# Last batch of a gated WKV and binary FFN: two groups' partial sums leave PSUM early, alpha within PSUM, biases regrouped

## The chip, the cores and the metric

The kernel runs on one core of one Trainium2 chip. The core has TensorE (matmuls, into PSUM), VectorE, ScalarE and GpSimd (elementwise work), and SyncE, which here only issues DMAs. GpSimd issues DMAs too; those that add into their destination go through it. Sixteen DMA engines serve all of them. The metric is the device time of one execution in microseconds (us); less is better. Times are medians of several runs. A profile is one further execution, recorded by the hardware profiler.

## The reference

Cut to what matters:

```python
# x, kv: (4, 1024, 1024); cond: (4, 256); w, u, bias: (1024,); weight: (1024, 1024); r = x, k = v = kv
tf    = sigmoid(sum(cond, -1))[:, None, None]
decay = exp(-exp(w)) * (0.5 + 0.5 * tf)
ek, ekv = exp(min(k, 30)), exp(min(k, 30)) * v
nf, df  = forward scans  a = a * decay + ekv,  b = b * decay + ek     # along the 1024 rows
nb, db  = the same backward
euk   = exp(min(u + k, 30))
base  = sigmoid(r) * (nf + nb - ekv + euk * v) / max(df + db - ek + euk, 1e-8)
gated = base * (0.8 + 0.2 * tf)
bw    = where(weight >= 0, 1, -1) * alpha       # alpha: mean |weight| of each output row
out   = x + gated @ bw.T + bias
```

## The kernel before

A step `g` is one batch and one block of 128 channels: 4 batches times 8 blocks are 32 steps (`steps`, 0 to 31). TensorE transposes the block so that channels lie on partitions; VectorE scans it forward and backward (L366, L379); ScalarE does exponentials and reciprocals; GpSimd and VectorE the products. The finished block is split into a rounded high part (`act_hi`, L433, ScalarE) and the remainder (`lo_part`, L438, GpSimd), and both are multiplied by the signs of the weights, `wT`. So every product counts two matmuls for each of the 8 blocks.

The order of every engine's work is written out by hand (`manual_schedule`): instructions stand on each engine's queue as they stand in the code, and an engine waits at the first whose inputs or buffers aren't ready. DMAs of SyncE and of GpSimd stand in those queues too.

The first three batches are multiplied channel block by channel block, turned back, put into `staged` tiles and stored. Their x is added afterwards by DMAs from GpSimd that accumulate from x in DRAM into the output in DRAM (`add_x`, L137 to L142, 1 MB each). Four of these twelve are left for the end (`adds[steps]`).

The last batch is multiplied the other way round: rows on partitions. It has 8 groups `n` of 128 rows, each with two halves (`part`) of 512 columns; one half takes 16 matmuls of 512 columns. Each group's x rows are loaded by `load_x_rows` (L477). Since a product over all 8 blocks needs the last step, most of it is left to the end, but the blocks that exist are multiplied as soon as PSUM has a bank for them: `pe_wide_product(n, part, blocks)` (L525). The banks come from `ps_o` (three of 512 columns), `ps_k`, `ps_g` (two each) and `bank`; groups 0 and 5 take both halves of the `ps_k` tile, group 3 of the `ps_g` tile, which also holds the transposed gate `sgT` of the step (L272). In step 30 two halves of group 1 get five blocks, in step 31 further groups get six.

After the last step's elementwise work (L801 to L818) the remaining two blocks follow for groups 0 to 3 (`waiting`, L822), and then groups 4 to 7 from the beginning. A finished half leaves PSUM by `leave_columns` (L536): VectorE multiplies it with `alpha_rows` into an SBUF tile `z` (L539) and adds this to the x rows (L541); then `dve_add_bias` (L530) adds `bias_rows` to a whole group, and SyncE stores it (`finish_wide`, L550). The last group goes in pieces of 512, 256 and 256 columns. `alpha_rows` and `bias_rows` are rows spread over all partitions by a DMA (`load_along_rows`, L494).

Buffers matter for the order of the loads: the gate pool has four tiles, which the x rows of some groups take over once TensorE has transposed their gate; the `eu` pool has three, which are free once the products of their step are done (the last with `num_product`, L419, of the last step's second half); `resid` has two (`staged` tiles). SyncE's queue at the end holds: bias_rows, x rows of groups 4, 5, 6, 7, then the stores. GpSimd's holds the two DMAs that add `euk` to `num` (L384), the product L419 of step 30, and the four `add_x`.

Of the kernel before, what the change touches and what calls it, by code (L numbers as in the profile page):

```python
# [9 lines left out]
F32 = mybir.dt.float32  # L10
# [11 lines left out]
def kernel(  # L22
# [27 lines left out]
    nc = tc.nc  # L50
    P = 128
    B, T, C = x.shape
    TD = time_emb.shape[1]
    NT = T // P
    NC = C // P
    H = 512
# [5 lines left out]
    rows = ctx.enter_context(tc.tile_pool(name="rows", bufs=2))  # L62
    gate_rows = ctx.enter_context(tc.tile_pool(name="gate_rows", bufs=4))
# [13 lines left out]
    sg_rows = {}  # L77
# [59 lines left out]
    def add_x(b, n):  # L137

        rows = slice(2 * n * P, 2 * (n + 1) * P)
        nc.gpsimd.dma_start(  # L140
            out=out[b, rows, :], in_=x[b, rows, :], accum_op=ALU.add, max_dma_last_dim=8192
        )  # L142
# [265 lines left out]
    def act_reciprocal(g, ts=slice(0, T)):  # L408
        b, cc = divmod(g, NC)
        rec = eus[g][:, ts]  # L410
        nc.scalar.activation(  # L411
            rec, rec, AF.Exp, scale=-1.0, bias=ln_g[:, b, cc : cc + 1]
        )
# [13 lines left out]
    def gated_product(g, ts=slice(0, T), engine=nc.gpsimd):  # L427
        engine.tensor_mul(nums[g][:, ts], dens[g][:, ts], nums[g][:, ts])  # L428
# [48 lines left out]
    def load_x_rows(n, pool, tag):  # L477
        t = pool.tile([P, C], F32, tag=tag, name=f"x_rows_{n}")
        nc.sync.dma_start(out=t, in_=x[last, n * P : (n + 1) * P, :])
        x_rows[n] = t  # L480
# [13 lines left out]
    def load_along_rows(pool, tag, name, values):  # L494
        t = pool.tile([P, C], F32, tag=tag, name=name)
        nc.sync.dma_start(out=t, in_=values.unsqueeze(0).to_broadcast([P, C]))
        return t
# [12 lines left out]
            t = ps_o.tile([P, H], F32, tag="po", name=f"wide_{n}_{part}")  # L510
            wide[n, part] = t

    def pe_wide_columns(t, n, cols, blocks):
        h, s = divmod(n, PER)
        for cc in blocks:
            for i in range(2):
                nc.tensor.matmul(  # L517
                    t,
                    gated[last, cc, h][:, i, s * P : (s + 1) * P],
                    wT[:, cc, cols],  # L520
                    start=(cc == 0 and i == 0),
                    stop=(cc == NC - 1 and i == 1),
                )

    def pe_wide_product(n, part, blocks):  # L525
        if (n, part) not in wide:
            open_wide(n, part)
        pe_wide_columns(wide[n, part], n, columns(part), blocks)

    def dve_add_bias(n):  # L530
        nc.vector.tensor_add(x_rows[n], x_rows[n], bias_rows)

    def columns(part):
        return slice(part * H, (part + 1) * H)

    def leave_columns(ps, n, cols):  # L536
        width = cols.stop - cols.start
        t = work.tile([P, width], F32, tag="z", name=f"wide_{n}_{cols.start}")
        nc.vector.tensor_mul(t, ps, alpha_rows[:, cols])  # L539
        xs = x_rows[n][:, cols]  # L540
        nc.vector.tensor_add(xs, xs, t)  # L541

    def leave_wide(n, part):
        leave_columns(wide[n, part], n, columns(part))

    def store_wide(n, part):
        rows = out[last, n * P : (n + 1) * P, columns(part)]
        nc.sync.dma_start(out=rows, in_=x_rows[n][:, columns(part)])

    def finish_wide(n):  # L550
        dve_add_bias(n)
        nc.sync.dma_start(out=out[last, n * P : (n + 1) * P, :], in_=x_rows[n])

    def act_leave(q):
        if q % 2 == 0:
# [61 lines left out]
    with tc.manual_schedule():  # L617
# [39 lines left out]
        def done():  # L657
            while fresh:
                ready.append(fresh.pop(0))

        def scale():
            while ready:
                scaled.append(ready.pop(0))
                act_scale(scaled[-1])

        def turn():
            if scaled:
                leaving.append(scaled.pop(0))
                pe_turn(leaving[-1])

        def leave():
            if leaving:
                act_leave(leaving.pop(0))

        for g in range(steps):
# [19 lines left out]
            if final:  # L695
                done()
            scale()
            done()
            if g > 1:
                act_hi(g - 2, 0)  # L700
                act_hi(g - 2, 1)
            product(parts[g][0])
            if final:
                pe_wide_product(2, 0, range(NC - 3))
            turn()
            if g > 0:
# [46 lines left out]
            leave()  # L753
            done()
            scale()
            if final:
                pe_wide_product(0, 1, range(NC - 2))
            product(parts[g][2])
            if g == steps - 2:
                pe_wide_product(1, 0, range(NC - 3))  # L760
            if g > 0:
                dve_newton_gate(g - 1)
            if g > 0 and not final:
# [7 lines left out]
                load_gate(g + 4)  # L771
            product(parts[g][3])
            turn()
            if parts[g][4]:
                done()
            product(parts[g][4])
            if g == steps - 2:
                pe_wide_product(1, 1, range(NC - 3))
            if final:
                gate = num_pool.tile([P, T], F32, tag="num", name="gate_of_last")  # L780
                nc.scalar.copy(gate, sg_ps[g])
                sg_ps[g] = gate
            leave()
            backward(g, dens[g], "edge_den")
            if not final:
# [4 lines left out]


        g = steps - 1
        bias_rows = load_along_rows(own, "euk", "bias_rows", bias)
        load_x_rows(4, gate_rows, "sg_rows")
        for i in adds[steps]:
            add_x(*i)

        for i in ((2, 1), (3, 0), (3, 1)):
            pe_wide_product(*i, range(NC - 2))

        for ts in halves:  # L801
            dve_denominator(g, ts)
# [2 lines left out]
            act_log(g, ts)  # L805
        for ts in halves:
            act_reciprocal(g, ts)
        gated_product(g - 1, engine=nc.vector)
        for h in range(NH):
            act_hi(g - 1, h)  # L810
        for h, ts in enumerate(halves):
# [4 lines left out]
            act_hi(g, h)  # L816
            lo_part(g - 1, h, nc.vector)
            lo_part(g, h, nc.vector)  # L818
        for n in range(5, NT):
            load_x_rows(n, eu_pool, "eu")  # L820

        waiting = [(n, part) for n in range(4) for part in range(2)]  # L822
        for i in waiting:
            pe_wide_product(*i, range(NC - 2, NC))
        for i in waiting:
            leave_wide(*i)
        biased = iter((0, 4, 1, 5, 2, 6, 3))
        for n in range(4, NT - 1):
            for part in range(2):
                pe_wide_product(n, part, range(NC))  # L830
                if n != 5:
                    leave_wide(n, part)
                    finish_wide(next(biased))

            for part in range(2 if n == 5 else 0):
                leave_wide(n, part)
                finish_wide(next(biased))
        dve_add_bias(NT - 1)
        finish_wide(next(biased))
        n = NT - 1  # L840
        for cols, pool, tag in (
            (slice(0, H), ps_o, "po"),
            (slice(H, 3 * H // 2), ps_o, "po"),
            (slice(3 * H // 2, C), ps_k, "kT"),
        ):
            bank_of = pool.tile([P, cols.stop - cols.start], F32, tag=tag, name=f"last_{cols.start}")
            pe_wide_columns(bank_of, n, cols, range(NC))
            leave_columns(bank_of, n, cols)
            nc.sync.dma_start(
                out=out[last, n * P : (n + 1) * P, cols], in_=x_rows[n][:, cols]  # L850
            )


# [28 lines left out]
```

## Time and profile before

| what | value |
|---|---|
| time, median of 3 runs | 489.85 us (489.81 to 491.19) |
| time of the profiled execution | 489.83 us |
| its span, first to last instruction | 488.0 us |
| VectorE busy | 474.9 us (97%) |
| GpSimd busy | 402.2 us (82%) |
| TensorE matmuls busy | 363.9 us (75%) |
| ScalarE busy | 335.9 us (69%) |
| DMA, SyncE's queue (q1) | 59.78 MB, 41.0% of 16 engines |
| DMA, GpSimd's queue (q0) | 29.37 MB, 31.6% of 16 engines |
| the 12 accumulating DMAs of 1 MB | 11.8 us from issue to landing (median) |

Shares are of the whole span. The time is 1.83 us more than the span. The page divides the span into stages only by its 40 slices; what happens in the last 60 us is read from the trace with a window: the chain of what ended last there, each engine's timeline, and the DMA queues' share of the 16 engines. An instruction's entry gives its start in us from the span's start, its length, its engine and line, and, in brackets, how long its engine stood idle before it and what ended that.

### The profile page before, as it was taken

What the parts mean: (1) busy time and instruction counts of PE and PEld (TensorE: products, weight loads), DVE (VectorE), ACT (ScalarE), POOL (GpSimd) and SP (SyncE); (2) the same over time, 40 slices, a digit from 0 to 9 for tenths busy, and PEclk for the clock granted to TensorE, in tenths of its full rate; (3) what the DMA queues carried; (4) which work ended last, traced back from release to release, by engine and by line L of the source; (5) the groups of instructions that cost most, each with busy time, mean ns of one, the idle gap of its engine ahead of it and who ended that gap; (6) DMA issues with size and microseconds to landing.
All of it is one profiled execution on the core that took longest, in us unless ns stands there. A gap on an engine that the chain in (4) does not pass through costs nothing.

```text
span 488.0 us, 5214 instructions
## 1 busy us (share of the span) xinstructions
PE 363.9 (75%) x1813; PEld 296.9 (61%) x1813; DVE 474.9 (97%) x331; ACT 335.9 (69%) x466; POOL 402.2 (82%) x276
## 2 busy tenths in 40 slices
PE   3434433344588877778999998965999998989996
PEld 2333332233466666656777777744888777868885
DVE  6999999999999999999999999999999999999976
ACT  4795968869595967769697879697866979724000
POOL 3379999999999999999999999999999999991000
PEclk9975566666699999999999999985999999999999
DMA  8865565555455555559787996889569697899954
GB/s 227 246 173 146 156 174 141 137 141 140 112 147 150 147 141 139 147 139 254 177 208 161 264 235 173 167 213 221 126 108 277 151 271 213 188 229 284 235 198 176
DMA packets 89762, 89.49 MB, mean 183 GB/s; under 512 B 2660, under 2 KB 80776, under 8 KB 88200
## 3 DMA queue, kind: packets, MB, share of 16 engines
q1 hardware_dynamic: 83320, 59.78, 41.0%
q0 software_dynamic: 6400, 29.37, 31.6%
q8 instruction: 14, 0.23, 0.2%
q14 instruction: 12, 0.10, 0.1%
q10 hardware_dynamic: 16, 0.00, 0.0%
HBM read 55.59 MB, written 29.36 MB: 174 GB/s over the span
## 4 chain that ended last, share of the span: by engine, by line
DVE 75%; PE 17%; issue 3%; ACT 2%; POOL 0%; DMA 0%; SPq 0%; DVEq 0%; POOLq 0%; ACTq 0%
DVE num L379 13%; DVE den L379 13%; DVE den L366 13%; DVE num L366 12%; PE wide L517 8%; DVE den L389 7%; DVE num L350 6%; DVE den L423 6%; PE po L449 5%; DVE euk L356 4%; PE last L517 2%; PE bank L517 1%; PE sgT L272 1%; PE turned L469 1%; PE kT L266 1%
## 5 line engine op out<-in xcount | busy, mean ns | idle before, releaser
L449 PE MATMUL po<-gated,wT 128*128 128x512 f32 x768 | 199.7, 408 | 0.3 <-ACT staged L557 0.3
L449 PEld LDWEIGHTS po<-gated,wT 128*128 128x128 f32 x768 | 141.9, 192 | 30.4 <-ACT staged L557 0.8
L266 PE MATMUL kT<-ident,k_rows 128*128 128x128 f32 x248 | 42.1, 325 | 61.6 <-issue 43.0
L272 PE MATMUL sgT<-ident,sg_rows 128*128 128x128 f32 x256 | 43.2, 324 | 46.4 <-DVE den L423 41.2
L438 POOL TENSOR_TENSOR gated<-num,gated 128x512 fp32r<-128x512 f32 x60 | 75.6, 1280 | 2.4
L266 PEld LDWEIGHTS kT<-ident,k_rows 128*128 128x128 f32 x248 | 33.8, 167 | 69.4 <-issue 51.6
L379 DVE TENSOR_TENSOR_SCAN den<-bank,edge_den,den 128x1024 f32<-128x1024 f32 x32 | 74.8, 2339 | 0.4 <-ACT edge_den L372 0.4
L416 POOL TENSOR_TENSOR den<-den,eu 128x1024 f32<-128x1024 f32 x31 | 73.8, 2380 | 1.4 <-ACT eu L411 1.4
L379 DVE TENSOR_TENSOR_SCAN num<-bank,edge_num,num 128x1024 f32<-128x1024 f32 x32 | 74.8, 2337 | 0.0
L419 POOL TENSOR_TENSOR num<-num,eu 128x1024 f32<-128x1024 f32 x31 | 73.7, 2377 | 0.8 <-DMA num<-euk 0.8
L428 POOL TENSOR_TENSOR num<-den,num 128x1024 f32<-128x1024 f32 x30 | 71.8, 2393 | 2.8 <-DVE den L423 0.5
L366 DVE TENSOR_TENSOR_SCAN den<-bank,den 128x1024 f32<-128x1024 f32 x32 | 72.2, 2258 | 0.0
L366 DVE TENSOR_TENSOR_SCAN num<-bank,num 128x1024 f32<-128x1024 f32 x31 | 70.6, 2277 | 0.0
L272 PEld LDWEIGHTS sgT<-ident,sg_rows 128*128 128x128 f32 x256 | 35.1, 167 | 57.1 <-DVE den L423 29.7
L433 ACT CAST gated<-num 128x512 fp32r<-128x512 f32 x64 | 36.5, 618 | 30.2 <-POOL num L428 25.8
L396 POOL TENSOR_SCALAR den<-den,floor 128x1024 f32<-128x1024 f32 x31 | 36.8, 1188 | 20.7 <-DVE den L389 17.5
L404 ACT ACTIVATE eu<-den,gain 128x1024 f32<-128x1024 f32 (+1 forms) x33 | 36.9, 1121 | 20.8 <-POOL den L396 20.4
L517 PE MATMUL wide<-wT,gated 128*128 128x512 f32 x192 | 45.4, 393 | 2.1 <-POOL gated L438 2.1
L557 ACT COPY staged<-turned 128x512 f32<-128x512 f32 x48 | 27.5, 574 | 21.3 <-PE turned L469 21.3
L517 PEld LDWEIGHTS wide<-wT,gated 128*128 128x128 f32 x192 | 35.8, 188 | 10.2 <-POOL gated L438 2.5
L389 DVE SCALAR_TENSOR_TENSOR den<-eu,top,den 128x1024 f32<-128x1024 f32 (+1 forms) x33 | 41.5, 1260 | 0.0
L356 DVE SCALAR_TENSOR_TENSOR euk<-eu,top,kT 128x1024 f32<-128x1024 f32 x31 | 38.7, 1250 | 0.0
(91 smaller groups left out, 578.9 us busy)
## 6 DMA issues: line engine op xcount, KB each, us to landing
sg_rows<-in_x_dram SPq DMA_DIRECT2D x32, 512.0 KB, 5.9
num<-euk POOLq DMA_DIRECT2D x32, 512.0 KB, 5.6
k_rows<-in_fside_BxSxS_dram SPq DMA_DIRECT2D x31, 512.0 KB, 5.2
out_dram<-staged SPq DMA_DIRECT2D x24, 512.0 KB, 5.1
out_dram<-in_x_dram POOLq DMA_DIRECT2D x12, 1024.0 KB, 11.8
w_rows<-in_L_ffn_weight_dram SPq DMA_DIRECT2D x8, 512.0 KB, 5.7
x_rows<-in_x_dram SPq DMA_DIRECT2D x8, 512.0 KB, 11.5
out_dram<-x_rows SPq DMA_DIRECT2D x7, 512.0 KB, 2.6
```

What stands on the lines that cost most here:

```text
L266: nc.tensor.transpose(kT[:, s * P : (s + 1) * P], k_rows[g][:, s, :], ident)
L272: nc.tensor.transpose(t[:, s * P : (s + 1) * P], sg_rows[g][:, s, :], ident)
L356: nc.vector.scalar_tensor_tensor(euk, eus[g], top[:, b, cc : cc + 1], k_ps[g], ALU.min, ALU.mult)
L366: nc.vector.tensor_tensor_scan(t, decay_row(g), t, 0.0, ALU.mult, ALU.add)
L379: nc.vector.tensor_tensor_scan(back, decay_row(g), back, inits[g, which], ALU.mult, ALU.add)
L389: nc.vector.scalar_tensor_tensor(dens[g][:, ts], eus[g][:, ts], top[:, b, cc : cc + 1], dens[g][:, ts], ALU.min, ALU.add,)
L416: engine.tensor_mul(dens[g][:, ts], dens[g][:, ts], eus[g][:, ts])
L419: engine.tensor_mul(nums[g][:, ts], nums[g][:, ts], eus[g][:, ts])
L428: engine.tensor_mul(nums[g][:, ts], dens[g][:, ts], nums[g][:, ts])
L438: engine.tensor_sub(t[:, 1, :], nums[g][:, h * H : (h + 1) * H], t[:, 0, :].bitcast(F32))
L449: nc.tensor.matmul(prods[q], wT[:, cc, oc * P : (oc + 1) * P], gated[b, cc, h][:, i, :], start=(cc == 0 and i == 0), stop=(cc == NC - 1 an ...
L517: nc.tensor.matmul(t, gated[last, cc, h][:, i, s * P : (s + 1) * P], wT[:, cc, cols], start=(cc == 0 and i == 0), stop=(cc == NC - 1 and i ...
```

## The change

Group 6 (`begun`) is multiplied in two parts. Five of its eight blocks (`pe_partial`, both halves) go into step 30; ScalarE copies each half into one SBUF tile `partial`, taken from `resid` (`act_partial`), so that the bank comes free. At the end GpSimd adds the bias to group 6's x rows, multiplies `partial` by alpha and adds it to the x rows; the four `add_x` DMAs stand behind these three in its queue. The other three blocks of group 6 are the last work of TensorE, in pieces of 512, 256 and 256 columns (`rest`). Other products of the early blocks move: (1, 0) within step 30, (1, 1) from step 30 to 31, (0, 1) behind the last gate transpose.

`leave_columns` multiplies by alpha within PSUM and adds from PSUM to the x rows. The other bias additions are put between the groups: 0 and 1 after (4, 0), 4 after (4, 1), 5 and 7 after group 5, 2 and 3 after (7, 0).

The copy of the last step's gate from PSUM (`gate_of_last`) moves behind the reciprocals on ScalarE. On SyncE's queue, group 6's x rows come ahead of group 4's; bias_rows, so far first, comes last, behind the x rows of 5 and 7, in the third `eu` tile, which group 7 had. The stores follow in the order 0, 1, 4, 5, 2, 3, 7, 6.

```diff
-    def pe_wide_columns(t, n, cols, blocks):
+    def pe_wide_columns(t, n, cols, blocks, ends=(0, NC - 1)):
...
-                    start=(cc == 0 and i == 0),
-                    stop=(cc == NC - 1 and i == 1),
+                    start=(cc == ends[0] and i == 0),
+                    stop=(cc == ends[1] and i == 1),
...
     def leave_columns(ps, n, cols):
-        width = cols.stop - cols.start
-        t = work.tile([P, width], F32, tag="z", name=f"wide_{n}_{cols.start}")
-        nc.vector.tensor_mul(t, ps, alpha_rows[:, cols])
+        nc.vector.tensor_mul(ps, ps, alpha_rows[:, cols])
         xs = x_rows[n][:, cols]
-        nc.vector.tensor_add(xs, xs, t)
+        nc.vector.tensor_add(xs, xs, ps)
...
+    begun = NT - 2
+    partial_ps = {}
+    partials = []
+
+    def pe_partial(part):
+        t = ps_o.tile([P, H], F32, tag="po", name=f"partial_{part}")
+        pe_wide_columns(t, begun, columns(part), range(NC - 3), (0, NC - 4))
+        partial_ps[part] = t
+
+    def act_partial(part):
+        if part == 0:
+            partials.append(resid.tile([P, C], F32, tag="x_res", name="partial"))
+        nc.scalar.copy(partials[0][:, columns(part)], partial_ps[part])
...
             scale()
+            if final:
+                act_partial(1)
             done()
...
             product(parts[g][0])
             if final:
+                pe_wide_product(1, 1, range(NC - 3))
                 pe_wide_product(2, 0, range(NC - 3))
...
-            if final:
-                pe_wide_product(0, 1, range(NC - 2))
             product(parts[g][2])
             if g == steps - 2:
-                pe_wide_product(1, 0, range(NC - 3))
+                pe_partial(0)
...
             turn()
+            if g == steps - 2:
+                leave()
+                act_partial(0)
+                pe_partial(1)
...
             if g == steps - 2:
-                pe_wide_product(1, 1, range(NC - 3))
-            if final:
-                gate = num_pool.tile([P, T], F32, tag="num", name="gate_of_last")
-                nc.scalar.copy(gate, sg_ps[g])
-                sg_ps[g] = gate
+                pe_wide_product(1, 0, range(NC - 3))
...
         g = steps - 1
-        bias_rows = load_along_rows(own, "euk", "bias_rows", bias)
-        load_x_rows(4, gate_rows, "sg_rows")
-        for i in adds[steps]:
-            add_x(*i)
-
-        for i in ((2, 1), (3, 0), (3, 1)):
-            pe_wide_product(*i, range(NC - 2))
+        for n in (begun, 4):
+            load_x_rows(n, gate_rows, "sg_rows")
...
             act_reciprocal(g, ts)
+        gate = num_pool.tile([P, T], F32, tag="num", name="gate_of_last")
+        nc.scalar.copy(gate, sg_ps[g])
+        sg_ps[g] = gate
+        for i in ((0, 1), (2, 1), (3, 0), (3, 1)):
+            pe_wide_product(*i, range(NC - 2))
...
-        for n in range(5, NT):
+        for n in (5, 7):
             load_x_rows(n, eu_pool, "eu")
+
+        bias_rows = load_along_rows(eu_pool, "eu", "bias_rows", bias)
+
+        def add_bias(n, engine=nc.vector):
+            engine.tensor_add(x_rows[n], x_rows[n], bias_rows)
...
+        add_bias(begun, nc.gpsimd)
+        nc.gpsimd.tensor_mul(partials[0], partials[0], alpha_rows)
+        nc.gpsimd.tensor_add(x_rows[begun], x_rows[begun], partials[0])
+        for i in adds[steps]:
+            add_x(*i)
...
-        biased = iter((0, 4, 1, 5, 2, 6, 3))
-        for n in range(4, NT - 1):
-            for part in range(2):
-                pe_wide_product(n, part, range(NC))
-                if n != 5:
-                    leave_wide(n, part)
-                    finish_wide(next(biased))
...
+        for n, part, biased in (
+            (4, 0, (0, 1)), (4, 1, (4,)), (5, 0, ()), (5, 1, (5, 7)), (7, 0, (2, 3)), (7, 1, ())
         ):
+            pe_wide_product(n, part, range(NC))
+
+            for i in ((0, 1) if part else ()) if n == 5 else (part,):
+                leave_wide(n, i)
+            for i in biased:
+                add_bias(i)
+                if i != 7:
+                    store_rows(i)
+        store_rows(7)
+        for cols in (slice(0, H), slice(H, 3 * H // 2), slice(3 * H // 2, C)):
+            t = ps_o.tile([P, cols.stop - cols.start], F32, tag="po", name=f"rest_{cols.start}")
+            pe_wide_columns(t, begun, cols, range(NC - 3, NC), (NC - 3, NC - 1))
+            leave_columns(t, begun, cols)
+            store_rows(begun, cols)
```

More of the change, by code (lines that the diff above doesn't have):

```diff
@@ L528, in pe_wide_product @@
         pe_wide_columns(wide[n, part], n, columns(part), blocks)
-    def dve_add_bias(n):
-        nc.vector.tensor_add(x_rows[n], x_rows[n], bias_rows)
     def columns(part):
@@ L536, in leave_columns @@
     def leave_columns(ps, n, cols):
-        width = cols.stop - cols.start
-        t = work.tile([P, width], F32, tag="z", name=f"wide_{n}_{cols.start}")
-        nc.vector.tensor_mul(t, ps, alpha_rows[:, cols])
+        nc.vector.tensor_mul(ps, ps, alpha_rows[:, cols])
         xs = x_rows[n][:, cols]
-        nc.vector.tensor_add(xs, xs, t)
+        nc.vector.tensor_add(xs, xs, ps)
     def leave_wide(n, part):
         leave_columns(wide[n, part], n, columns(part))
[L546 to L552, printed above, removed]
+    begun = NT - 2
[9 more added lines that the diff above has]
+        nc.scalar.copy(partials[0][:, columns(part)], partial_ps[part])
     def act_leave(q):
@@ L818, with store_rows @@
             lo_part(g, h, nc.vector)
-        for n in range(5, NT):
+        for n in (5, 7):
             load_x_rows(n, eu_pool, "eu")
+        bias_rows = load_along_rows(eu_pool, "eu", "bias_rows", bias)
+        def add_bias(n, engine=nc.vector):
+            engine.tensor_add(x_rows[n], x_rows[n], bias_rows)
+        def store_rows(n, cols=slice(0, C)):
+            nc.sync.dma_start(
+                out=out[last, n * P : (n + 1) * P, cols], in_=x_rows[n][:, cols]
+            )
+        add_bias(begun, nc.gpsimd)
[3 more added lines that the diff above has]
+            add_x(*i)
         waiting = [(n, part) for n in range(4) for part in range(2)]
@@ L826 @@
             leave_wide(*i)
-        biased = iter((0, 4, 1, 5, 2, 6, 3))
-        for n in range(4, NT - 1):
-            for part in range(2):
-                pe_wide_product(n, part, range(NC))
-                if n != 5:
-                    leave_wide(n, part)
-                    finish_wide(next(biased))
[L835 to L844, printed above, removed]
-        ):
[L846 to L851, printed above, removed]
+        for n, part, biased in (
+            (4, 0, (0, 1)), (4, 1, (4,)), (5, 0, ()), (5, 1, (5, 7)), (7, 0, (2, 3)), (7, 1, ())
+        ):
+            pe_wide_product(n, part, range(NC))
[11 more added lines that the diff above has]
+            store_rows(begun, cols)
 _INS = [
```

## The prediction

> **What bounds the kernel now.** The page's chain first: over the whole span it lies on VectorE, so a change at the end must be judged from the end alone. Then the chain for the last stretch, cut into pieces (start us, length us, what).
>
> ```profile
> 437.53 0.87 PE sgT L272 x8
> 438.40 2.76 PE bank L517 x12
> 441.16 9.16 PE wide L517 x40
> ...
> 452.15 23.80 PE wide L517 x104
> 475.95 7.44 PE last L517 x48
> ...
> 483.88 0.42 DVE x_rows L541
> ```
>
> From 430.6 on TensorE never pauses: 104 matmuls of 512 columns take 23.80 us, 0.229 each, and what is counted in them ends the run. VectorE is close behind; its timeline shows one real pause:
>
> ```profile
> 464.24 1.23 DVE L531 TENSOR_TENSOR x_rows<-x_rows,bias_rows 128x1024 f32<-128x1024 f32 x1
> 468.67 0.69 DVE L539 TENSOR_TENSOR wide<-wide,alpha_rows 128x512 f32<-128x512 f32 x1 [3.20 <-PE wide L517]
> ```
>
> That wait is for both halves of group 5, which share a PSUM tile. Next, what SyncE and GpSimd issue before it:
>
> ```profile
> 435.77 0.33 SPq L496 DMA_DIRECT2D bias_rows<-in_L_ffn_bias_dram  x1
> 436.19 11.29 SPq L479 DMA_DIRECT2D x_rows<-in_x_dram  x4
> ```
> ```profile
> 435.83 2.40 POOL L419 TENSOR_TENSOR num<-num,eu 128x1024 f32<-128x1024 f32 x1 [0.85 <-DMA num<-euk]
> 438.17 3.45 POOL L140 DMA_DIRECT2D out_dram<-in_x_dram  x4
> ```
>
> The last x load is issued at 447.15 (the four end at 447.48): it waits until VectorE's num L419 lets the third `eu` tile go. The four accumulating DMAs (1 MB each) leave GpSimd's queue from 438.17. Last the DMA engines: stretches (busy us per engine, clock, DMA share, GB/s), then the two queues in 442.8 to 466.7 and in 464.9 to 488.
>
> ```profile
> 449.00:459.00 10.00, 10.00 (x45) 8.22 (x44) 9.67 (x16) 0.07 (x1) 0.00 (x0) 1.00 1.05 249
> 459.00:464.00 5.00, 5.00 (x24) 4.10 (x23) 4.90 (x8) 0.00 (x0) 0.00 (x0) 1.00 1.04 216
> 464.00:468.00 4.00, 4.00 (x19) 3.28 (x18) 1.43 (x2) 0.00 (x0) 0.00 (x0) 1.00 0.94 311
> 468.00:472.00 4.00, 4.00 (x19) 3.29 (x18) 3.27 (x5) 0.00 (x0) 0.00 (x0) 1.00 0.06 25
> 472.00:482.00 10.00, 10.00 (x56) 8.65 (x55) 9.83 (x12) 0.00 (x0) 0.00 (x0) 1.00 0.52 212
> 482.00:486.00 4.00, 1.38 (x12) 1.18 (x11) 2.06 (x5) 0.00 (x0) 0.00 (x0) 1.00 0.69 257
> ```
> ```profile
> q0 software_dynamic: 575, 4.19, 84.6%
> q1 hardware_dynamic: 467, 1.68, 18.5%
> ```
> ```profile
> q1 hardware_dynamic: 1440, 4.19, 45.9%
> ```
>
> All 16 DMA engines are full until 466. The four accumulations (q0, 4.19 MB) take 84.6% of 23.9 us: 20.2 us of all engines. The stores (4.19 MB) take 45.9% of 23.1 us: 10.6 us. Together the queues reach 103.5%: the engines serve one by making the other wait. After 468 they have room; the last store finds them free.
>
> **The change, part by part.** The profiled execution has a span of 488.0 us and a time of 489.83, 1.83 around it, and the median of the runs is 489.85: the sum starts there.
>
> *TensorE.* 20 matmuls (five blocks of group 6, both halves) go into step 30, and (0, 1)'s 12 go from before the last sgT transpose to behind it. Group (1, 1)'s ten move into step 31, where TensorE stood 2.10 us for GpSimd's gated L438. The added ten fill that pause, and 12 leave ahead of the transpose, so it starts at about 437.3, as now. Behind it stand 48 + 32 + 96 + 12 = 188 matmuls of 512 columns instead of 36 + 32 + 96 + 32 = 196: 8 x 0.229 = 1.8 us less, last matmul at 481.3, 1.9 sooner by its own count.
>
> *ScalarE.* Two 128x512 copies out of PSUM, 0.57 each by staged L557. The first reuses the tile of a store that was issued at 419.09 and landed 6.5 later, 425.6; ScalarE is free at 424.3. The gated casts behind it move from 425.73 to about 426.9 and end at 428.0; GpSimd's L438 needs them at 429.29, so nothing follows. TensorE's (1, 0) takes the bank that the first copy empties at 426.2 and waits half a us for it, time that it has. A store landing over 1.3 us later would hand the excess to TensorE and VectorE: at 10.1 us, as the `num` DMA beside it, 2.3; no gain either way. The copy of the last gate (1.02) moves behind the reciprocals, which end at 442.46: VectorE's L423 starts at 443.45 instead of 443.10, plus 0.35.
>
> *VectorE.* One bias addition goes to GpSimd. Groups 5 and 7 and the rest follow group 5's second half, which TensorE ends at 438.2 + 144 x 0.229 = 471.2 (468.4 now, four matmul groups later). From about 471.4 VectorE has four pairs (mul and add, 1.32 apart: 449.72 to 451.04), four biases (1.14 apart: 461.66 to 462.80) and the last 3.1 (481.04 to 484.30 less its 0.18 wait): 12.9, ending at 484.3, as before (484.30). The pause is not filled, it only comes later and longer. Mul within PSUM has no row: from 1.14 a pair (two halves of a 1024-wide addition) to 1.44 (both starts 0.72 apart), so 1.1 us less to 0.7 more over the six pairs' worth; I take 1.32, since the present mul reads PSUM already.
>
> *SyncE.* The x loads of groups 6, 4, 5 and 7 now meet no accumulations and land sooner; VectorE's first use of x is at 450, so nothing is won. Group 6's load goes ahead of the `num` DMA's arrival (it landed 10.1 us after issue, and L419 waited 0.85): one more 512 KB load is 1.3 us of the engines, and L419 would end at 439.5. VectorE's num L428, which needs it, starts at 440.18: hidden, 0.6 us short of showing. The bias moves from the first place to the last: it takes the `eu` tile that the fourth x load has now, so it's issued at 447.15 + 0.35 = 447.5. A 512 KB store in free engines lands 2.6 us after issue, x_rows under load 5.0: it lands between 450.1 and 452.5, and I take 450.1, as the engines are empty there without accumulations.
>
> *GpSimd.* Bias addition, alpha product and x addition, each 128x1024, stand in its queue ahead of the four accumulations. By L416, L419 and L428 they take 2.38 to 2.39 each: 7.2, ending at 457.3. VectorE wants the sum only near 481. But behind the wait for the bias stand the accumulations, which nobody waits for except the end of the program: they leave at 457.3 instead of 438.17. First packets come 1.5 us after issue at best (a `num` DMA at 411.83, nothing before 413.2), 4.7 at worst (442.8 now, engines full); I take 1.6, since the engines are empty: 458.9.
>
> *DMA engines, the sum.* From 458.9 stand 20.2 + 10.6 = 30.8 us of work and no pause: the first store is issued at about 463, the last at 484.3, inside the backlog. At 103.5% that is 29.8 us, to 488.7; at 100%, 489.7. Today's last packet is at about 485.7, 2.3 before the span ends: 491.0 to 492.0, against 488.0, plus 3.0 to 4.0. I take the middle: 489.83 + 3.5 = **493.3**. Bounds: a bias 2.4 late and first packets 3.1 late give 498.8; 103.5% throughout gives 492.8, and a bias landing as fast as the smallest store (1.9 us) 492.1.
>
> *A rule against it.* The Trainium skill's page "DMA: Bandwidth & Descriptors", section "Anatomy of one DMA — SWDGE (gpsimd) path", gives a GpSimd-issued DMA about 2.0 us plus bytes over 436e3 per us. By that the four accumulations are 9.6 us of transfer instead of 20.2, the backlog is gone before 484, and the time would stay at 489.8. The rows above show the same four at half that rate, alone as well (459 to 464: 1.04 of the engines, 216 GB/s), so I go by the rows.
>
> **The rivals.**
> 1. *No change, 489.8.* The accumulations are hidden after all, and VectorE's 484.3 ends the run as now. For it: nothing computes on them, and the engines have 8.6 us of idle share between 468 and 482. It decides if the DMA work is over by 485.7: accumulations starting before 455.9, or 3 us of stores served beside them for nothing. Against: the 103.5%, and three GpSimd instructions behind a load that can't be issued before 447.
> 2. *Faster, 487.7.* TensorE's end at 481.3 decides: two additions of 0.43 and the 3.7 from the last addition to the end (484.30 to 488.0) give 485.9 + 1.83. VectorE would have to lose 2 us of its 12.9, twice what the lower bound of a pair gives, with the DMAs hidden too.
> 3. *Slower still, 495 to 498.* GpSimd's three wait for a late bias, or ScalarE's copy for the store; every us passes through to the accumulations or to VectorE. For it: x_rows loads took 11.5 and more today; against: that was beside the accumulations.
>
> **How the numbers follow.** Forecast 0.70 (its own range 491.6 to 495), rival 3 0.09, rival 1 0.13, rival 2 0.08. A measurement here tells about 0.3% from no change, 1.5 us: under 488.4 is faster, over 491.3 slower. Faster: 0.08; same: 0.13 and 0.02 of the forecast's low edge, 0.15; slower: 0.77. The range takes in most of the no-change case and of rival 3: 489.4 to 497.0.
>
> **What would show it.** In the profile after: bias_rows issued near 447.5; three GpSimd L828, L836, L837 near 450 to 457; L140 from about 457; DMA share near 1.0 from 459 to 488, and stores landing 10 us or more after issue instead of 2.6; TensorE ending near 481.3 and VectorE near 484.3 with a pause near 467 to 471; the chain ending in a DMA. It is wrong if L140 starts much sooner, if the DMA share falls under 0.9 before 480, or if a wide pause on ScalarE near 425 reaches TensorE.

## The result, and the profile after

The changed kernel takes 495.75 us (median of 4 runs, 495.3 to 496.04) against 489.98 us before (median of 4, 489.81 to 491.19): a ratio of 1.0112, 95% interval 1.0093 to 1.013. It is slower. The profiled execution took 495.94 us, with a span of 494.2 against 488.0 before: 6.2 us more. One thing must be known for the comparisons below: the kernel before takes either about 489.8 or about 491.3 us, and two of the experiments either about 490.8 or about 492.3, for a cause that stays open, since only the shorter ones were traced; all of these runs count in the medians and in the ratios, which are all to the kernel before.

Begin where the prediction said the cost would be, in GpSimd's timeline of the kernel after (start us, length us, engine, line, operation, and in brackets the idle time ahead of it with what ended that):

```profile
451.35 2.42 POOL L828 TENSOR_TENSOR x_rows<-x_rows,bias_rows 128x1024 f32<-128x1024 f32 x1 [13.10 <-DMA bias_rows<-in_L_ffn_bias_dram]
453.73 2.40 POOL L836 TENSOR_TENSOR partial<-partial,alpha_rows 128x1024 f32<-128x1024 f32 x1
456.21 2.41 POOL L837 TENSOR_TENSOR x_rows<-x_rows,partial 128x1024 f32<-128x1024 f32 x1
458.57 3.37 POOL L140 DMA_DIRECT2D out_dram<-in_x_dram  x4
```

GpSimd stands idle for 13.10 us until the bias lands, works 7.2 us, and only then issues the four accumulations, at 458.57: 20.4 us later than before. SyncE's timeline gives the load that it waited for, and the ten stores at the end:

```profile
447.46 0.33 SPq L496 DMA_DIRECT2D bias_rows<-in_L_ffn_bias_dram  x1
464.54 20.58 SPq L831 DMA_DIRECT2D out_dram<-x_rows  x10
```

The stretches of the end (length, then busy time of PE, PEld, DVE, ACT and POOL, granted clock, DMA share, GB/s) show what became of it:

```profile
450.00:457.00 7.00, 7.00 (x32) 5.77 (x31) 5.87 (x10) 0.00 (x0) 5.57 (x3) 1.00 0.03 10
457.00:462.00 5.00, 5.00 (x23) 4.10 (x22) 4.83 (x9) 0.00 (x0) 4.94 (x5) 1.00 0.42 79
462.00:468.00 6.00, 6.00 (x28) 4.92 (x27) 5.90 (x8) 0.00 (x0) 0.00 (x0) 1.00 1.01 198
468.00:474.00 6.00, 6.00 (x28) 4.91 (x27) 2.93 (x5) 0.00 (x0) 0.00 (x0) 1.00 1.05 251
474.00:480.00 6.00, 6.00 (x29) 4.97 (x28) 5.93 (x8) 0.00 (x0) 0.00 (x0) 1.00 1.00 246
480.00:486.00 6.00, 1.54 (x11) 1.13 (x10) 4.20 (x9) 0.00 (x0) 0.00 (x0) 1.00 0.99 286
486.00:490.00 4.00, 0.00 (x0) 0.00 (x0) 0.00 (x0) 0.00 (x0) 0.00 (x0) 0.51 1.02 416
490.00:494.20 4.20, 0.00 (x0) 0.00 (x0) 0.00 (x0) 0.00 (x0) 0.00 (x0) 0.50 0.30 110
```

From 450 to 457 the DMA engines do nothing (0.03), where before they were full. From 462 to 490 they are full, and behind 486 no engine computes at all: only stores are served, at 416 GB/s. Full until 490 and 0.30 of the last 4.2 us means that the bulk of the work is over at about 491.3 (behind it come 27 small packets, 0.03 MB, the last near 492.3); the span ends 2.9 us after 491.3. The two queues in 455 to 493, 38 us:

```profile
q0 software_dynamic: 576, 4.19, 55.4%
q1 hardware_dynamic: 1440, 4.19, 28.1%
```

Those are 21.1 us of all engines for the accumulations and 10.7 for the stores, 31.7 together, in the 31.2 us from the first packets (about 460.1) to 491.3.

VectorE ends where it ended before. Its timeline has the long pause ahead of group 5 and the last instruction:

```profile
471.20 0.70 DVE L534 TENSOR_TENSOR wide<-wide,alpha_rows 128x512 f32<-128x512 f32 x1 [2.97 <-PE wide L517]
...
483.98 0.42 DVE L536 TENSOR_TENSOR x_rows<-x_rows,rest 128x256 f32<-128x256 f32 x1
```

It is over at 484.40 (484.30 before). And here is a trap in the reading. The chain that ended last, of the kernel after, ends in

```profile
483.98 0.42 DVE x_rows L536
```

just as it did before, though the run now goes on for 9.8 us behind this instruction instead of 3.7. The chain follows engines; the backlog of the DMA engines is not in it. Only the stretches show it.

### The profile page after: what moved, and what is told of

The parts are those of the page before. It is cut to its first block, busy times and chain, and to the rows that moved or that the text cites. A ratio compares the mean times of both kernels' runs of the same rounds, so it can differ in the third digit from the quotient of the medians.

```text
span 494.2 us, 5196 instructions
## 1 busy us (share of the span) xinstructions
PE 364.0 (74%) x1803; PEld 296.2 (60%) x1803; DVE 474.2 (96%) x330; ACT 337.4 (68%) x468; POOL 409.7 (83%) x279
## 4 chain that ended last, share of the span: by engine, by line
DVE 79%; PE 12%; issue 3%; ACT 2%; DMA 0%; SPq 0%; DVEq 0%; ACTq 0%
DVE num L379 14%; DVE den L379 13%; DVE den L366 13%; DVE num L366 12%; DVE den L389 7%; DVE den L423 6%; DVE num L350 6%; PE wide L517 5%; PE po L449 5%; DVE euk L356 4%; DVE x_rows L828 1%; DVE x_rows L536 1%; PE turned L469 1%; PE kT L266 1%; ACT den L278 1%
## 5 line engine op out<-in xcount | busy, mean ns | idle before, releaser
L419 POOL TENSOR_TENSOR num<-num,eu 128x1024 f32<-128x1024 f32 x31 | 73.7, 2377 | 0.9 <-DMA num<-euk 0.9
```

Source lines behind the costliest of these rows:

```text
L419: engine.tensor_mul(nums[g][:, ts], nums[g][:, ts], eus[g][:, ts])
```

## The experiments

Two theories stood at the start. **Theory:** the accumulations, held back behind GpSimd's three instructions, make the DMA engines end last, and nothing else in the change costs time. **Rival:** another part costs it: the longer pause of VectorE, ScalarE's two copies, the product within PSUM, or the work on GpSimd itself.

### Accumulations first

The one edit to the changed kernel is the order on GpSimd:

```diff
+        for i in adds[steps]:
+            add_x(*i)
         add_bias(begun, nc.gpsimd)
         nc.gpsimd.tensor_mul(partials[0], partials[0], alpha_rows)
         nc.gpsimd.tensor_add(x_rows[begun], x_rows[begun], partials[0])
-        for i in adds[steps]:
-            add_x(*i)
```

> The changed kernel with one thing put back: the four accumulating DMAs stand ahead of GpSimd's three instructions for group 6, as before the change (issued near 438 instead of 458.6). Theory (the delayed accumulations fill the DMA engines until after the last store): the accumulations are done near 467 again, the stores find free engines, VectorE's last addition near 484.4 ends the run, span about 488.1, time 489.9 (489.4 to 490.8; the bias then lands near 459 beside the accumulations, which GpSimd's three and VectorE's first bias at 463 can take). Rival (the other parts of the change cost the time: the copies on ScalarE, the mul within PSUM, the new order of the groups): the time stays near 495.8.

It took 489.63 us (489.5 to 490.33, 10 runs), a ratio of 0.9977 (0.9964 to 0.9989) and 6.1 us less than the changed kernel. The theory holds: this order is the whole loss, and the rest of the change costs nothing on balance. One reading was new, in VectorE's timeline:

```profile
463.29 4.06 DVE L828 TENSOR_TENSOR x_rows<-x_rows,bias_rows 128x1024 f32<-128x1024 f32 x2
...
471.19 0.70 DVE L534 TENSOR_TENSOR wide<-wide,alpha_rows 128x512 f32<-128x512 f32 x1 [1.25 <-PE wide L517]
```

Two bias additions that took 2.35 us in the changed kernel take 4.06 here. The bias now lands late, beside the accumulations, so GpSimd's three run from 457.87 to 465.14, over the start of these additions. The pause ahead of group 5 takes up the loss (1.25 instead of 2.97), so the time doesn't show it.

### Without the accumulations

```diff
         nc.gpsimd.tensor_add(x_rows[begun], x_rows[begun], partials[0])
-        for i in adds[steps]:
-            add_x(*i)
```

> The changed kernel without the four accumulating DMAs of the end; it leaves out the addition of x for the 1024 rows of the third batch. Theory: as with the first of these runs, VectorE ends the run, span about 488.1, time 489.9, the DMA share after 460 near 0.5. If the other parts of the change cost something, the time stays above 492 although the DMA engines are free. If the accumulations had been hidden, nothing changes against 495.8.

This kernel leaves out the addition of x to the 1024 rows of the third batch. Measured: 489.55 us (489.51 to 489.69, 10 runs), ratio 0.9977 (0.9966 to 0.9988). Taking the accumulations away entirely is worth no more than issuing them early (489.63). So, issued early, they are hidden completely, and what is left is VectorE's end at 484.4 and the last store.

### Accumulations behind one of the three

```diff
         add_bias(begun, nc.gpsimd)
-        nc.gpsimd.tensor_mul(partials[0], partials[0], alpha_rows)
-        nc.gpsimd.tensor_add(x_rows[begun], x_rows[begun], partials[0])
         for i in adds[steps]:
             add_x(*i)
+        nc.gpsimd.tensor_mul(partials[0], partials[0], alpha_rows)
+        nc.gpsimd.tensor_add(x_rows[begun], x_rows[begun], partials[0])
```

> The changed kernel with the four accumulations behind the first of GpSimd's three instructions (the bias addition) instead of the third: they start 4.8 us sooner (two instructions of 2.4 us), near 453.8. Theory: the DMA engines' backlog starts 4.8 us sooner and ends 4.8 us sooner, time 495.75 - 4.8 = 491.0 (490.4 to 491.6). Rival (only their place behind the late bias counts, or the other parts of the change): 495 or more. If VectorE ended the run instead, 489.9.

Measured: 491.07 us (490.69 to 491.46, 10 runs), ratio 1.0005 (0.9993 to 1.0017).

```profile
453.41 3.39 POOL L140 DMA_DIRECT2D out_dram<-in_x_dram  x4
```

They are issued 5.16 us sooner than in the changed kernel (453.41 against 458.57), and the time is 4.68 us shorter: 0.91 us for each. Drawn on at this rate, the loss against the order of the first experiment (6.12) is gone at an issue near 451.8, an estimate.

### The kernel before with its accumulations late

GpSimd takes the biases of three groups, and the accumulations go behind it; no partial sum, no product within PSUM, the old order on TensorE.

```diff
     def dve_add_bias(n):
-        nc.vector.tensor_add(x_rows[n], x_rows[n], bias_rows)
+        if n < 5:
+            nc.vector.tensor_add(x_rows[n], x_rows[n], bias_rows)
...
         load_x_rows(4, gate_rows, "sg_rows")
-        for i in adds[steps]:
-            add_x(*i)
...
+        for n in (7, 5, 6):
+            nc.gpsimd.tensor_add(x_rows[n], x_rows[n], bias_rows)
+        for i in adds[steps]:
+            add_x(*i)
```

> The kernel before with the accumulations delayed alone: GpSimd adds the bias to groups 7, 5 and 6 (three instructions of 128x1024, 7.2 us; the first waits for the last x load, issued at 447.2), and the four accumulations stand behind them, near 458. VectorE leaves out these three bias additions; nothing else of the change is in it, and the output is the same. Theory: the DMA engines are full from about 460 to 491 as in the changed kernel, time 495.0 (493.8 to 496.2), though VectorE has 3.4 us less to do. Rival (the delay itself is hidden, the rest of the change costs): 489.9 or less.

Measured: 497.65 us (496.47 to 498.01, 4 runs), ratio 1.0133 (1.011 to 1.0156). The direction is the theory's; the size is over what was expected, and the profiled execution is the lowest of the four (496.47), so that a part of it stays open. In that execution the DMA engines are what ends last again: their share is 1.02 from 486 to 490, and VectorE is over at 484.96. GpSimd's three biases took longer than three times 2.4, and VectorE beside them more than that. GpSimd's timeline, then VectorE's:

```profile
450.60 8.29 POOL L822 TENSOR_TENSOR x_rows<-x_rows,bias_rows 128x1024 f32<-128x1024 f32 x3 [12.57 <-DMA x_rows<-in_x_dram]
458.85 3.37 POOL L140 DMA_DIRECT2D out_dram<-in_x_dram  x4
```

```profile
450.94 0.68 DVE L540 TENSOR_TENSOR wide<-wide,alpha_rows 128x512 f32<-128x512 f32 x1
451.65 2.17 DVE L542 TENSOR_TENSOR x_rows<-x_rows,wide 128x512 f32<-128x512 f32 x1
...
460.08 0.69 DVE L542 TENSOR_TENSOR x_rows<-x_rows,wide 128x512 f32<-128x512 f32 x1
```

The product, which reads one SBUF tile and one PSUM bank, stays at 0.68. The addition to x, which in the old form reads two SBUF tiles, takes 2.17, 2.16 and 2.19 while GpSimd works and 0.69 when it is done: 4.5 us lost in three additions. The DMA engines stood still meanwhile (share 0.00 from 450 to 458), so they are not the cause. In the changed kernel the addition reads PSUM, and beside the same GpSimd work every one of them took 0.69. The Trainium skill's page "SBUF — State Buffer", section "Who interferes with whom", says that a VectorE instruction with two SBUF inputs contends with a GpSimd instruction that reads SBUF, and that one with at most one SBUF input, outside VectorE's 2-port modes, does not; the 2.17 and the 0.69 agree.

### Bias early, accumulations still behind the three

The bias gets back its own tile and its first place; GpSimd's three could then begin some 8 us sooner.

```diff
         g = steps - 1
+        bias_rows = load_along_rows(own, "euk", "bias_rows", bias)
         for n in (begun, 4):
             load_x_rows(n, gate_rows, "sg_rows")
...
-        bias_rows = load_along_rows(eu_pool, "eu", "bias_rows", bias)
```

> The changed kernel with the bias load back in its old place (first of SyncE's loads, near 435.6, into its own tile, landing near 441.4) and the accumulations still behind GpSimd's three instructions. Theory: the three run from about 441.5 to 449.5 and the accumulations start near 450, so that they and the stores are done near 483 and VectorE ends the run: 489.6. On top, GpSimd's three lie beside VectorE's last products, which read two SBUF tiles; in the fourth run such additions took 2.17 us instead of 0.69 beside GpSimd. About three of them would put VectorE 4 us back, of which its pauses of 0.95 and 2.97 us take most: 489.6 to 491.5. Rival (the wait for the bias isn't what makes the accumulations late): 494 or more.

Measured: 494.1 us (493.89 to 494.32, 4 runs), ratio 1.0079 (1.0062 to 1.0096): a miss. The DMA share is only 0.61 in 474 to 480 and 0.60 in 480 to 486, so they are not what ends last here. The time is the one that the rival named, but not for its reason: the accumulations were issued at 450.89, 7.7 us sooner than in the changed kernel. VectorE ends last: GpSimd now works from 442.98 to 450.9, beside VectorE's last products of two SBUF tiles.

```profile
443.34 2.59 DVE L423 SCALAR_TENSOR_TENSOR den<-den,gate_of_last 128x512 f32<-128x512 f32 x1 [0.22 <-ACT gate_of_last L808]
445.96 2.78 DVE L428 TENSOR_TENSOR num<-den,num 128x512 f32<-128x512 f32 x1
448.66 3.44 DVE L438 TENSOR_TENSOR gated<-num,gated 128x512 fp32r<-128x512 f32 x2
```

In the changed kernel the same lines took 0.69, 0.69 and 1.46: 6.0 us lost, and VectorE ended at 488.36 instead of 484.40. So the late bias was not only a cost: it held GpSimd off until VectorE was past the instructions that it would have blocked.

### Biases in VectorE's pause

With the accumulations first, the order of the first experiment, VectorE ends last, and its pause ahead of group 5 is worth filling. Two versions: the biases of groups 2 and 3 behind (4, 1) as well, and all five there.

```diff
-            (4, 0, (0, 1)), (4, 1, (4,)), (5, 0, ()), (5, 1, (5, 7)), (7, 0, (2, 3)), (7, 1, ())
+            (4, 0, (0, 1)), (4, 1, (4, 2, 3)), (5, 0, ()), (5, 1, (5, 7)), (7, 0, ()), (7, 1, ())
```

> The first run (accumulations first) with the bias additions and stores of groups 2 and 3 moved from behind (7, 0) to behind (4, 1), into VectorE's pause for group 5. Theory: with the accumulations out of the way VectorE's work after group 5 sets the end; 2.3 us of it move into a pause of 1.25 us (the first run shows the rest of the old pause taken by two bias additions that stand beside GpSimd's three), so the end comes 1.2 us sooner: 488.4. Rival (TensorE's end near 482 sets the run): 489.6, no gain.

```diff
-            (4, 0, (0, 1)), (4, 1, (4,)), (5, 0, ()), (5, 1, (5, 7)), (7, 0, (2, 3)), (7, 1, ())
+            (4, 0, ()), (4, 1, (0, 1, 4, 2, 3)), (5, 0, ()), (5, 1, (5, 7)), (7, 0, ()), (7, 1, ())
```

> As the run before, and the bias additions of groups 0 and 1 move from behind (4, 0) to behind (4, 1) too, so that five bias additions (5.7 us) stand between 465.3 and 471.1, after GpSimd's three (457.9 to 465.1), and none beside them. Theory: no addition is stretched, VectorE reaches group 5 without delay and ends about 1.4 us sooner than in the first run, limited by TensorE's (7, 1) near 478.4: 488.1 (487.8 to 488.6), faster than both kernels. Rival: the stores, now later, run into each other at the end: 489.6 or more.

The first took 489.06 us (488.42 to 491.21, 10 runs), ratio 0.9984 (0.9971 to 0.9998); the second 488.98 (488.01 to 491.11, 12 runs), ratio 0.9977 (0.9962 to 0.9992). Both scatter by some 3 us, where the first experiment's ten runs lie within 0.83. The fastest reach what was expected, the medians don't. The profiled executions show a reason. In that of the first version the bias lands so late that GpSimd's three run from 462.77 to 471.9, beside VectorE's first two additions:

```profile
463.36 6.26 DVE L828 TENSOR_TENSOR x_rows<-x_rows,bias_rows 128x1024 f32<-128x1024 f32 x2
```

6.26 us instead of 2.35. In that of the second, GpSimd starts at 461.22 and five additions take 8.59 instead of 5.7. How much GpSimd overlaps with the additions hangs on when the bias lands beside the accumulations. That this makes the scatter is argued from one profile each, not shown.

### The old way out of PSUM

The order of the first experiment, with the product written to SBUF as before the change:

```diff
+        width = cols.stop - cols.start
+        t = work.tile([P, width], F32, tag="z", name=f"wide_{n}_{cols.start}")
-        nc.vector.tensor_mul(ps, ps, alpha_rows[:, cols])
+        nc.vector.tensor_mul(t, ps, alpha_rows[:, cols])
         xs = x_rows[n][:, cols]
-        nc.vector.tensor_add(xs, xs, ps)
+        nc.vector.tensor_add(xs, xs, t)
```

> The first run (accumulations first) with the old way of leaving PSUM: the product with alpha goes to SBUF, and the addition to x reads two SBUF tiles. Theory: mul and add take the same 1.33 us a pair where GpSimd is idle, but beside GpSimd's three (457.9 to 465.1) about three additions take 2.17 us instead of 0.69, and VectorE's pause of 1.25 us doesn't hold that: 491 to 493. Rival (the place of the product makes no difference): 489.6.

Measured: 491.13 us (490.35 to 491.88, 10 runs), ratio 1.002 (1.0008 to 1.0033), where the product in PSUM gave 0.9977 (in another comparison): some 1.5 us to 2 us more. The stretch is there again: beside GpSimd (458.07 to 466.1) three additions were stretched, the first of them

```profile
458.32 2.70 DVE L538 TENSOR_TENSOR x_rows<-x_rows,wide 128x512 f32<-128x512 f32 x1
```

The three took 2.70, 2.18 and 2.19, the others 0.69; VectorE ended at 485.80 instead of 484.40. Without GpSimd beside them the two forms cost VectorE nearly the same: most pairs take 1.32 to 1.34 us in both.

### GpSimd kept away from VectorE's two-tile instructions

If that is so, GpSimd's three belong between VectorE's last products (until 450.1) and its first bias additions (463.3), where VectorE reads one SBUF tile at a time. The accumulations go first, the bias is loaded early, its addition comes last on GpSimd, and the product goes into a `num` tile that was expected to come free at the right moment:

```diff
+        bias_rows = load_along_rows(own, "euk", "bias_rows", bias)
...
+        for i in adds[steps]:
+            add_x(*i)
+        scaled = num_pool.tile([P, C], F32, tag="num", name="scaled")
+        nc.gpsimd.tensor_mul(scaled, partials[0], alpha_rows)
+        nc.gpsimd.tensor_add(x_rows[begun], x_rows[begun], scaled)
+        add_bias(begun, nc.gpsimd)
...
+            (4, 0, (0, 1)), (4, 1, (4, 2, 3)), (5, 0, ()), (5, 1, (5, 7)), (7, 0, ()), (7, 1, ())
```

> The changed kernel with the accumulations first, the bias load in its old early place, GpSimd's three in the order product, addition, bias, where the product goes into a `num` tile that VectorE lets go near 449.4, and the bias additions of groups 2 and 3 behind (4, 1). So GpSimd works from about 449.5 to 457, beside VectorE's pairs, which read one SBUF tile each, and nothing it does waits for a late load. Theory (two causes, both seen in the runs before: late accumulations, and additions on VectorE stretched where both engines read two SBUF tiles): both are gone, the pause of 2.97 us takes 2.3 us of biases, the end is 1.4 us before that of the first run: 488.1 (487.8 to 488.5), with little scatter, where the run with five biases in the pause scattered from 488.0 to 491.1. Rival (the stretch comes from something else, such as the DMAs): VectorE's additions in 449 to 457 or 463 to 471 are stretched again, 489 to 491.

Measured (this kernel is called e9 below): 492.28 us (490.61 to 492.8, 12 runs), ratio 1.0024 (1.0009 to 1.0038): a miss. The tile came free too soon, at 448.0, when VectorE had read the last gate out of it. GpSimd began at 448.11, half a microsecond ahead of VectorE's last two low parts:

```profile
448.62 5.72 DVE L438 TENSOR_TENSOR gated<-num,gated 128x512 fp32r<-128x512 f32 x2
```

instead of 1.46. So VectorE came out of them 4.3 us late. TensorE did not stand for the low parts themselves, but for a bank: VectorE began to empty the banks at 454.26, where the version that cures this (e11, below) began at 451.01, and TensorE waited 2.01 us, until 458.51. VectorE's pauses took up a part, and its last addition ended at 485.27, against 484.40 in the changed kernel, in an execution of 490.77 us. A variant with the rest of group 6 ahead of (7, 1) was run beside it:

```diff
-            (4, 0, (0, 1)), (4, 1, (4, 2, 3)), (5, 0, ()), (5, 1, (5, 7)), (7, 0, ()), (7, 1, ())
+            (4, 0, (0, 1)), (4, 1, (4, 2, 3)), (5, 0, ()), (5, 1, (5, 7)), (7, 0, ())
...
-        store_rows(7)
+        store_rows(7, slice(0, H))
+        for n, cols, blocks in (
+            (begun, slice(0, H), range(NC - 3, NC)), (begun, slice(H, C), range(NC - 3, NC)),
+            (7, slice(H, 3 * H // 2), range(NC)), (7, slice(3 * H // 2, C), range(NC)),
+        ):
```

> As the run before, with group 6's rest (two halves of 512 columns) ahead of (7, 1), which goes last in two pieces of 256 columns. TensorE's long matmul groups then end later than the rest's short ones, and VectorE has less behind the last: TensorE's end near 481.4, one pair of 0.87 us behind it, 482.3 instead of 483.0 for VectorE's last addition. Theory: 487.4 (487.0 to 487.9). If VectorE's backlog rather than TensorE's end limits the stretch, no gain against the run before: 488.1.

Measured: 492.07 us (490.72 to 492.3, 12 runs), ratio 1.0019 (1.0005 to 1.0032), with the same stretch (5.71 us). Nothing on the order can be read from it.

The stretch suggests the cure: write the product into the tile that the last low part itself reads, so that GpSimd has to come behind it.

```diff
-        scaled = num_pool.tile([P, C], F32, tag="num", name="scaled")
-        nc.gpsimd.tensor_mul(scaled, partials[0], alpha_rows)
-        nc.gpsimd.tensor_add(x_rows[begun], x_rows[begun], scaled)
+        nc.gpsimd.tensor_mul(nums[g], partials[0], alpha_rows)
+        nc.gpsimd.tensor_add(x_rows[begun], x_rows[begun], nums[g])
```

> The arrangement of e9 with one change: GpSimd's product goes into the numerator tile of the last step itself, which VectorE's last low part reads, so that GpSimd cannot begin ahead of it. Theory (VectorE stands behind a GpSimd instruction wherever it reads two SBUF tiles): the last two low parts take 1.46 us again in place of 5.72, GpSimd runs from about 450.1 for three times 2.4 us beside VectorE's pairs with one SBUF tile, which stay at 0.69, VectorE ends some 4 us before e9's and the time is 488.1 us (487.6 to 488.9). Rival (the stretch of e9 had another cause, such as the early bias load): the low parts stay long and the time stays at 490.8 to 492.3 us.

Measured (this kernel is called e11): 488.37 us (488.24 to 488.6, 6 runs), ratio 0.9957 (0.9941 to 0.9973). GpSimd's timeline, then VectorE's:

```profile
450.13 2.40 POOL L836 TENSOR_TENSOR num<-partial,alpha_rows 128x1024 f32<-128x1024 f32 x1 [8.57 <-DVE gated L438]
...
455.09 2.40 POOL L827 TENSOR_TENSOR x_rows<-x_rows,bias_rows 128x1024 f32<-128x1024 f32 x1
```

```profile
448.58 1.47 DVE L438 TENSOR_TENSOR gated<-num,gated 128x512 fp32r<-128x512 f32 x2
...
466.96 3.50 DVE L827 TENSOR_TENSOR x_rows<-x_rows,bias_rows 128x1024 f32<-128x1024 f32 x3
471.14 0.70 DVE L534 TENSOR_TENSOR wide<-wide,alpha_rows 128x512 f32<-128x512 f32 x1 [0.69 <-PE wide L517]
...
482.51 0.42 DVE L536 TENSOR_TENSOR x_rows<-x_rows,rest 128x256 f32<-128x256 f32 x1
```

The low parts are back at 1.47, GpSimd's three at 2.40, three biases fill the pause, and VectorE ends at 482.93, 1.5 us sooner than in the changed kernel and 2.3 sooner than in e9; the profiled executions, 488.44 and 490.77 us, differ by the same 2.3. The early bias load was kept from e9, so it wasn't the cause of the stretch. The six runs lie within 0.36 us.

The variant with the rest of group 6 ahead of (7, 1), built on this one:

> The product in the last step's own numerator tile as in e11, and the rest of group 6 ahead of the second half of group 7. Theory: as e11, and the whole-row store of group 6 leaves ahead of the last one, so that the wait of TensorE for the bank of (7, 1) goes: 487.4 us (486.8 to 488.6). Rival (the order of the last products does not matter, as between e9 and e10): the same as e11 within 0.3 us.

Measured: 488.25 us (488.21 to 488.35, 6 runs), ratio 0.9955 (0.994 to 0.9969). Its order is worth 0.1 us, so the rival holds there. Both versions beat the kernel before and the changed one; against the lower of the two times of the kernel before (489.64 to 489.8 in that comparison) the gain is about 1.4 us.

## Why the prediction was right, and where its sizes were off

The direction and the mechanism held: the accumulations were held back, the DMA work ended last, and putting them first took the loss away. The time came out 2.45 us over the forecast of 493.3, inside the range (489.4 to 497.0), but 0.75 outside the forecast's own (491.6 to 495): the rise was 5.8 us where 3.5 was forecast. To lie in the wide range says little, since it begins below the time before; the pieces say more. The term that was mis-sized most is the landing of the bias. Step by step:

- **GpSimd and the bias.** The bias was issued at 447.46 (predicted 447.5) but landed 3.7 us later, not 2.6, and GpSimd began at 451.35 instead of 450.1. This is the largest mis-sized term, 1.25 us, and it lies within the bound of 452.5. The three instructions took the 7.2 us that were taken, and the first packets came 1.6 us after the issue, as taken. First packets near 460.1 instead of 458.9: **+1.2**.
- **DMA engines.** Predicted were 30.8 us of work, in 29.8 to 30.8 us. Measured: 31.7 us of work in 31.2, because the accumulations took 21.1 instead of 20.2. Against the middle, 30.3: **+0.9**. The two queues together reached 102%, between the 100% and the 103.5% that bounded the sum (of the 103.5, 0.4 belonged to two other queues).
- **From the last packet to the end.** 2.3 was taken from the last packet of the kernel before; here the span ends 2.9 us after the bulk of the work, 1.9 after the last small packet: **+0.6**. Together 2.7 us on the predicted span of 491.5, which is the measured 494.2.
- **The rule against it.** The Trainium skill's page "DMA: Bandwidth & Descriptors", section "Anatomy of one DMA — SWDGE (gpsimd) path", made 9.6 us of transfer of the four accumulations and so no change. They took 21.1 us of all 16 engines here; the measurement decides, and the rows were the better guide.
- **TensorE.** The transpose began at 436.78 (predicted 437.3). The last matmul ended at 482.4 instead of 481.3: the last six waited 0.89 us for the bank of (7, 1), which VectorE had not emptied. Not foreseen, and hidden.
- **VectorE.** It ended at 484.40 (predicted 484.3), with a pause of 2.97 us ahead of group 5; most pairs took 1.33 and some 1.45, where 1.32 was taken. That its end came out within 0.1 us is in part luck, for it also paused 0.95 us ahead of its first pair: (0, 1)'s twelve matmuls, moved behind the transpose, made the first banks later (451.06 instead of 449.72). The prediction counted those matmuls for TensorE's end and not for VectorE's start; the pause ahead of group 5 covered it.
- **ScalarE.** Copies at 425.38 for 1.19 us, casts done by 427.6 (predicted 428.0), the late gate copy moved VectorE's L423 to 443.40 (predicted 443.45): as told.
- **SyncE.** L419 was not delayed: it ended at 438.25, not 439.5. It was priced as hidden in any case.
- **What was not priced at all.** The prediction took GpSimd's 7.2 us as free for VectorE. In the changed kernel that is so, but only because the new way out of PSUM leaves one SBUF input to each VectorE instruction there; with the old one the three additions beside GpSimd took 2.18 to 2.70 instead of 0.69. That condition should have been in the text.
- **What would show it.** The chain did not end in a DMA, as the text said it would; the stretches carried the finding alone.

The rivals: *no change* fell, since the stores were not served beside the accumulations for nothing. Its turning point, first packets before 455.9, was too late: in the third experiment they came at 455.2, and the time was still 1.4 us over that of the first. By that experiment's slope the point lies near an issue at 451.8, with 1.6 to 1.8 us to the first packet near 453.5, an estimate. *Faster* fell for the changed kernel; its condition, VectorE over sooner with the DMAs hidden, is what e11 then brought about, by another arrangement, at 488.37. *Slower still* named the late bias: that alone was 1.25 us of the 2.7, and the measured 495.75 lies at the low end of its 495 to 498. Its other half, a late copy on ScalarE, did not occur.

## What to carry to other kernels

When work is put ahead of a DMA on the queue that issues it, price the DMA's own path: how much all the engines have left to move, from when, and whether something behind it fills the rest; every microsecond past the turning point here cost 0.91, by two runs. Look at the DMA share of the last stretches, not at the chain, to see a backlog. And before giving work to GpSimd, list VectorE's instructions beside it by how many SBUF tiles they read: a product kept in PSUM was worth some 1.5 to 2 us here, and a tile chosen so that GpSimd starts behind the last of the two-tile instructions 2.3 us between the profiled executions (3.9 between the medians).

## What the runs showed of the hardware that was not expected

- VectorE instructions with two SBUF inputs stood behind GpSimd instructions that read SBUF: a 128x512 addition took 2.16 to 2.70 us instead of 0.69, a pair of 128x1024 bias additions 4.06 to 6.26 instead of 2.35, a pair of low parts 3.44 to 5.72 instead of 1.46. In the first experiment the pair of bias additions began at 463.29 and ended at 467.35, 2.21 us behind the end of GpSimd's last instruction (465.14): about the 2.35 that it takes alone, so it did next to nothing until GpSimd was done. GpSimd was stretched too, 2.40 to as much as 3.40 (3.65 beside the issue of the accumulations). VectorE instructions with one SBUF input and one PSUM input kept their 0.69 beside the same GpSimd work.
- An accumulation of 1 MB from DRAM to DRAM took about 5.3 us of all 16 engines (21.1 for four), twice the 2.7 us that as many bytes of plain stores took (10.7 for the same 4.19 MB).
- The bias, a row spread over all partitions (512 KB written) by idle DMA engines, landed 3.7 us after its issue, where a store of 512 KB had taken 2.6.
